# Where a division and an inverse root stand in a TensorE-bound transformer block

## The chip, the cores and the metric

The kernel runs on one core of one Trainium2 chip. The metric is the device time of one execution in microseconds, the median of several runs. A core has TensorE (PE, with its weight loads shown apart as PEld), VectorE (DVE), ScalarE (ACT) and GpSimd (POOL), each with an instruction queue that runs in order, and SyncE (SP), which here only issues transfers.

## The reference

A transformer block with conditioning, in fp32, on x of 4 sequences of 1024 tokens with 512 features; 16 heads of 32, a hidden width of 2048. `g` and `b` are linear in a conditioning vector of 128 per sequence.

```
norm(x) = g * x * rsqrt(mean(x*x) + 1e-6) + b
x1  = x + attention(norm1(x))          # softmax(q k^T / sqrt(32)) v, then Wo
ref = x1 + (silu(n @ gate^T) * (n @ hid^T)) @ out^T     with n = norm2(x1)
out = x + ref
```

What matters below: the softmax is divided by its row sums after the product with v, and norm2 needs the inverse root of one mean per token.

## The kernel before

Everything is held transposed: features on the 128 partitions, tokens along the rows. Tokens come in 8 blocks of 512 (two to a sequence). For each block there are 4 groups of 4 heads and 2 halves of 256 queries: 64 jobs `j`. A job takes 4 slots, each for 256 of the 1024 keys. So the main loop (L774) runs over 256 slots `g` plus 12 to drain, 32 slots to a block; `kind` is g mod 4, and in this text a slot's *place* is g mod 32.

The order of the work is written out by hand: inside the loop each engine's instructions stand in the order in which the calls are made, and the scheduler leaves the four compute engines alone. SyncE's transfers are placed by the framework. Three lists hang further work into slots: `pin` at a slot's start, `between` and `amid` in its middle, `after` at its end.

A job is a pipeline over several slots. `scores` (L316) puts a slot's scores into PSUM; `keep` (L323, ACT) copies them out; `running_max` (L328, L331, DVE) takes the maxima. At the next slot of kind 0, `max_T` (L337) transposes the maxima and `parts` (L343 to L348, DVE) reduces them to one per query. At the slot of kind 1 behind it, `parts_T` (L353, tile pt, then a copy L355) turns them, and `spread` (L363, tile sp, then copies L364 to `shift`) puts them on all partitions. `shifted` (L369, DVE) subtracts, `exponential` (L372, ACT) takes exp in place, one slot later `weighted` (L382, tile av) multiplies with v, and `accumulate` (L396) adds the slot's exponentials to the job's first by a transfer that GpSimd issues. When a job's four are summed, at the next slot of kind 0, `fold_sum` (L404) and `sums` (L414) give the row sums, `sums_out` (L419) copies them out as `total`, `inverse` (L422) takes their reciprocal on VectorE and `normalize` (L431) multiplies the job's output by it into oT.

From slot FS = 60 on, the feed-forward part (FFN) runs beside the attention of the next blocks, one hidden group `p` to two slots. Its products are pairs into two PSUM banks, a (tile pa) and b (tile pb): `pair_26`, `filler` (the output product pc of earlier groups, 4 x 512 columns), `pair_7` in even slots; `pair_3`, `pair_15` of the next group and `pair_4` in odd ones. On VectorE `take_contract` (L583) adds pc to the residual in `res`, which frees pc's bank; `sub_5` (L552) and `add_15` (L530) combine products; `gate` and `hidden` make h. Tiles pa, pc, sum, pt and sp all come from the pool `ps`, tag w, which has two banks.

The second norm of a block (tag f) takes squares (L138 to L144), a mean over features by TensorE (`norm_mean`, in the slot e + 17), and then an inverse root on few values: each of 512 tokens has one value on all 128 partitions, so `compact` writes one row to DRAM, `take` reads it back as 128 x 4 (tile few), `root` (L173, ACT, Sqrt) and `invert` (L177, DVE) work on that, and `put` and `norm_spread` bring it back to all partitions through DRAM. `norm_scale` (L199) and `norm_mod` (L202) then scale x. e is the block's first slot for block 0, and four slots before it for the others, so that e + 20 is place 20 there and place 16 here.

The diff touches the end of the loop's body, where a job is divided:

```
906            if n_on and j_n < direct and kind in (0, 2):
909                at = g - kind
910                in_first = j_n % GB == GB - 1 or (at >= FS and at % BS not in (12, 24, 28))
911                if in_first == (kind == 0):
912                    inverse(j_n)
914                    if j_n != GB:
915                        normalize(j_n)
```

j_n is the job whose sums are due, GB = 8 jobs and BS = 32 slots to a block. In the FFN's slots this puts the division into the slot of kind 0, but two slots later for the jobs due at places 12, 24 and 28 (so at places 14, 26 and 30). The last two jobs are divided in `take_sums`.

Of the kernel before, what the change touches and what calls it, by code (L numbers as in the profile page):

```python
# [9 lines left out]

F32 = mybir.dt.float32
BF16 = mybir.dt.bfloat16
AF = mybir.ActivationFunctionType
ALU = mybir.AluOpType
# [3 lines left out]
P = 128  # L18
# [6 lines left out]
def tile_cond_transformer_block(  # L25
# [13 lines left out]
    nc = tc.nc  # L39
    NBLK, _, C, _ = x.shape  # L40
# [17 lines left out]
    sb = ctx.enter_context(tc.tile_pool(name="sb", bufs=1))  # L58
# [14 lines left out]
    eps = const.tile([P, 1], F32, tag="eps", name="eps")  # L73
# [42 lines left out]
    y, wkq, wv, wo, kq, v = {}, {}, {}, {}, {}, {}  # L116
# [3 lines left out]
    state = {}  # L120
# [30 lines left out]
    def norm_mean(tag: str, inside: bool):  # L151
        if inside:
            pm = ps_av.tile([P, NB], F32, tag="av", name=f"pm{tag}")
        else:
            pm = ps.tile([P, NB], F32, tag="w", name=f"pm{tag}")
        mm(pm, ones_mean, state[tag], True, True)
        nc.scalar.copy(state[tag], pm)

    def compact(tag: str, t, rows: int, n: int):

# [3 lines left out]
    def take(tag: str):  # L164

        src = inv_s.pop(tag)
        few = sb.tile([P, src.shape[0] * src.shape[1] // P], F32, tag="few", name=f"few{tag}", bufs=2)
        nc.sync.dma_start(out=few, in_=src.rearrange("h (p c) -> (h p) c", c=few.shape[1]))
        state["few", tag] = few

    def root(tag: str):
        few = state["few", tag]
        nc.scalar.activation(few, few, AF.Sqrt, bias=eps)  # L173

    def invert(tag: str):
        few = state["few", tag]
        nc.vector.reciprocal(few, few)  # L177

    def put(tag: str):
        few = state.pop(("few", tag))  # L180
# [144 lines left out]
    def running_max(r: int, k: int):  # L325
        j, u = divmod(r, UN)
        if u:
            nc.vector.tensor_tensor(rmax[j], rmax[j], raw[r][:, k, :, :], ALU.max)  # L328
        elif k:
            rmax[j] = sb.tile([P, HG, HQ], F32, tag="rmax", name=f"rmax{j}")  # L330
            nc.vector.tensor_tensor(rmax[j], raw[r][:, 0, :, :], raw[r][:, 1, :, :], ALU.max)  # L331
# [74 lines left out]
    def take_av(j: int):  # L406
        avs[j] = sb.tile([P, HQ], F32, tag="avs", name=f"avs{j}", bufs=2)
        nc.scalar.copy(avs[j], av.pop(j))
# [12 lines left out]
    def inverse(j: int):  # L421
        nc.vector.reciprocal(state["total", j], state["total", j])  # L422

    def normalize(j: int):

        m, qh = divmod(j, NB // HQ)
        n, hg = divmod(m, C)
        total = state.pop(("total", j))
        if (n, hg) not in oT:
            oT[n, hg] = sb.tile([P, NB], F32, tag=f"oT{hg}", name=f"oT{m}")  # L430
        nc.vector.tensor_tensor(oT[n, hg][:, qh * HQ : (qh + 1) * HQ], avs.pop(j), total, ALU.mult)  # L431
# [157 lines left out]
    GB = C * (NB // HQ)  # L589
    BS = GB * UN  # L590
# [15 lines left out]
    def after(g, fn, *a):  # L606
        ended.setdefault(g, []).append((fn, a))
# [21 lines left out]
    for b in range(1, B):  # L629
        for half in range(QB):  # L630
            s = math.ceil((len(queue) + 1) / PACE)
            s4 = s - 4 - (s - 6) % UN
            tag = f"a{b}_{half}"
# [10 lines left out]
    FS = BS + 28  # L644
# [3 lines left out]
    for n in range(NBLK):  # L648
        g0 = (n + 1) * BS
        pin(g0 + 6, load_res, n)  # L650
        e = g0 if n == 0 else g0 - 4
        go = e + 13 if n < NBLK - 1 else g0 + 8
        for d in range(C):
            first.append((go, None, project_out, (n, d)))
            pin(go - 3 + (d // 2 * 4 if n else 0), load_wo, n, d)
        if n < NBLK - 1:
            tag = f"f{n}"
            after(e + 16, add_res, n)
            for k in range(2):
                after(e + 15 + k, lambda n=n, tag=tag, k=k: norm_squares(x2[n], tag, k))  # L660
            if n == 0:
                between(e + 17, norm_mean, tag, False)
            else:
                amid.setdefault(e + 17, []).append((norm_mean, (tag, True)))
            after(e + 17, norm_compact, tag)
            after(e + 19, take, tag)
            after(e + 20, root, tag)
            after(e + (20 if n == 0 else 21), invert, tag)
            after(e + (21 if n == 0 else 22), put, tag)
            after(e + (22 if n == 0 else 24), norm_spread, tag)  # L670
            scales, mods = ((24, 24, 25, 25), (25, 25, 26, 26)) if n == 0 else ((22, 22, 24, 24), (23, 23, 25, 25))
            for c in range(C):
                after(g0 + scales[c], lambda n=n, tag=tag, c=c: norm_scale(x2[n], tag, c))
                between(g0 + mods[c], lambda n=n, c=c: norm_mod(1, n // QB, x2[n], c))
            for i in range(4):
                after(g0 + (26, 26, 27, 28)[i] - (n > 0 and i == 0), token_sums, n, i)
# [27 lines left out]
    with tc.manual_schedule(  # L704
# [69 lines left out]
        while g < END:  # L774
# [40 lines left out]
                keep(g)  # L815
            if kind == 1 and s_on:
                take_av(j_s)
            due = bool(first) and first[0][0] <= g
            if not ffn:
                if x_on:  # L820
                    exponential(r_x)
                evict = chain(g, FG)
                if kind == 0:
                    take_sums(j_n)
                if g < NR:
                    running_max(g, 0)
                    running_max(g, 1)
                if kind == 0 and m_on:
                    columns[0] = P
                    max_T(j_m)  # L830
                    parts(j_m)
                if evict is not None:
                    evict()
                for fn, a in halfway.pop(g, []):
                    fn(*a)
                if g == FS - 1:
                    columns[0] = DH
                    pair_15(0)
                    take_5(0)
                    add_15(0)  # L840
                elif even:
                    late = chain(g, FG)
                if g in (FS - 4, FS - 2):
                    load_f((g - FS + 4) // 2)
            elif even:
                load_f(p + 2)
                pair_26(p)
                copy_156(p)
                if kind == 0:
                    take_sums(j_n)  # L850
                if x_on:
                    exponential(r_x)
                if kind == 0 and m_on:
                    max_T(j_m)
                    parts(j_m)
                one, two, evict = filler(p)
                one()
                two()
                if g < NR:
                    running_max(g, 0)  # L860
                    running_max(g, 1)
                if evict is not None:
                    evict()
                pair_7(p)
                sub_5(p)
                for fn, a in halfway.pop(g, []):
                    fn(*a)
            else:
                extra = due or len(queue) > FG
                evict = None  # L870
                if kind == 3 and extra:
                    evict = chain(g)
                pair_3(p)
                if kind == 3:
                    gate_tanh(p)
                if x_on:
                    exponential(r_x)
                pair_15(p + 1)
                take_5(p + 1)
                for fn, a in amid.pop(g, []):  # L880
                    fn(*a)
                if kind == 1:
                    gate_tanh(p)
                    if extra:
                        spare_bank[0] = True
                        evict = chain(g)
                if g < NR:
                    running_max(g, 0)
                if kind == 3 and evict is not None:
                    evict()  # L890
                if kind == 3:
                    gate(p)
                if g < NR:
                    running_max(g, 1)
                add_15(p + 1)
                if kind == 1:
                    gate(p)
                    if evict is not None:
                        evict()
                pair_4(p)  # L900
                hidden(p)
                if due:
                    chain(g)()
                for fn, a in halfway.pop(g, []):
                    fn(*a)
            if n_on and j_n < direct and kind in (0, 2):


                at = g - kind
                in_first = j_n % GB == GB - 1 or (at >= FS and at % BS not in (12, 24, 28))  # L910
                if in_first == (kind == 0):
                    inverse(j_n)

                    if j_n != GB:
                        normalize(j_n)
            columns[0] = DH
            for fn, a in ended.pop(g, []):
                fn(*a)
# [93 lines left out]
```

## Time and profile before

| | us |
|---|---|
| median of 3 runs (lowest, highest) | 2449.82 (2447.05, 2451.08) |
| the profiled execution | 2455.29 |
| its span in the trace | 2453.4 |
| four slots from place 4 on in the FFN (slots 100 to 103) | 29.6 |
| mean granted TensorE clock | 0.994 |

A slot's length is the distance of the first score matmul (L316) from the one of the slot before. In the profile, lines are those of the kernel before. A row of the timeline gives start and length in us, engine, line, operation, the tiles it writes and reads, and how many instructions are merged; brackets hold the idle time of that engine before it and what ended it. The start-up before the first slot takes 50.5 us; the FFN's tail without attention runs from about 2190 to the end.

### The profile page before, as it was taken

What the parts mean: (1) busy time and instruction counts of PE and PEld (TensorE: products, weight loads), DVE (VectorE), ACT (ScalarE), POOL (GpSimd) and SP (SyncE); (2) the same over time, 40 slices, a digit from 0 to 9 for tenths busy, and PEclk for the clock granted to TensorE, in tenths of its full rate; (3) what the DMA queues carried; (4) which work ended last, traced back from release to release, by engine and by line L of the source; (5) the groups of instructions that cost most, each with busy time, mean ns of one, the idle gap of its engine ahead of it and who ended that gap; (6) DMA issues with size and microseconds to landing.
All of it is one profiled execution on the core that took longest, in us unless ns stands there. A gap on an engine that the chain in (4) does not pass through costs nothing. (4 is left out here: it accounts for less than half of the span.)

```text
span 2453.4 us, 72677 instructions
## 1 busy us (share of the span) xinstructions
PE 2385.5 (97%) x32553; PEld 1135.9 (46%) x32553; DVE 1940.7 (79%) x2183; ACT 1413.2 (58%) x1495; POOL 172.4 (7%) x207
## 2 busy tenths in 40 slices
PE   8999999999999999999999999999999999999999
PEld 3333334344444544544454544454445445444444
DVE  2688888878799988998899979997999799843332
ACT  3677776765566656665566656665666566512110
POOL 0000000000000000000000000000000000000000
PEclk9999999999999999999999999999999999999999
DMA  6599999988788788889888888898788888853442
GB/s 216 166 304 259 256 258 240 231 202 219 198 205 210 188 226 209 208 207 229 204 200 213 225 197 209 204 230 207 198 207 203 224 200 204 198 165 117 140 131 70
DMA packets 185988, 501.79 MB, mean 205 GB/s; under 512 B 21319, under 2 KB 78663, under 8 KB 158286
## 3 DMA queue, kind: packets, MB, share of 16 engines
q0 software_dynamic: 28656, 208.68, 43.9%
q1 hardware_dynamic: 156734, 288.47, 35.4%
q8 instruction: 256, 4.19, 0.7%
q14 instruction: 54, 0.44, 0.1%
q10 hardware_dynamic: 288, 0.01, 0.0%
HBM read 246.44 MB, written 41.97 MB: 118 GB/s over the span
## 5 line engine op out<-in xcount | busy, mean ns | idle before, releaser
L369 DVE TENSOR_TENSOR raw<-raw,shift 128x2048 f32<-128x2048 f32 (+1 forms) x320 | 588.8, 1857 | 25.6 <-ACT shift L364 25.6
L323 ACT COPY raw<-sc 128x2048 f32<-128x2048 f32 x256 | 479.7, 1874 | 187.4 <-PE sc L316 130.8
L372 ACT ACTIVATE raw<-raw 128x2048 f32<-128x2048 f32 x256 | 490.8, 1917 | 157.1 <-DVE raw L369 154.8
L328 DVE TENSOR_TENSOR rmax<-rmax,raw 128x1024 f32<-128x1024 f32 x384 | 469.5, 1223 | 48.8 <-ACT raw L323 42.2
L112 PE MATMUL pc<-h,ow 128*32 128x512 f32 x4096 | 470.5, 596 | 5.2 <-DMA ow<-in_out_w 4.2
L382 PE MATMUL av<-raw,v 128*32 128x256 f32 x4096 | 271.9, 383 | 35.6 <-ACT raw L372 35.1
L396 POOL DMA_DIRECT2D raw<-raw x192 | 165.3, 861 | 1967.4 <-ACT raw L372 878.9
L316 PE MATMUL sc<-q,k 32*128 32x256 f32 x4096 | 293.3, 400 | 1.0 <-ACT raw L323 1.0
L112 PE MATMUL pa<-x,fa 128*32 128x256 f32 x4096 | 272.5, 384 | 4.1 <-DVE pa L530 4.1
L112 PE MATMUL pa<-sums,fw 128*32 128x256 f32 x4096 | 271.5, 383 | 0.0
L112 PEld LDWEIGHTS pc<-h,ow 128*32 128x32 f32 x4096 | 128.6, 110 | 250.7 <-issue 231.9
L316 PEld LDWEIGHTS sc<-q,k 32*128 32x128 f32 x4096 | 184.9, 184 | 117.4 <-issue 75.8
L112 PE MATMUL pkq<-y,wkq 128*32 128x512 f32 (+1 forms) x1664 | 232.5, 594 | 4.3 <-ACT y L202 4.1
L112 PEld LDWEIGHTS pa<-x,fa 128*32 128x32 f32 x4096 | 124.7, 110 | 119.7 <-DVE pa L530 21.4
L382 PEld LDWEIGHTS av<-raw,v 128*32 128x32 f32 x4096 | 110.4, 109 | 149.4 <-ACT raw L372 66.0
L112 PEld LDWEIGHTS pa<-sums,fw 128*32 128x32 f32 x4096 | 134.4, 111 | 90.0 <-issue 3.4
L583 DVE SCALAR_TENSOR_TENSOR res<-pc,res 128x512 f32<-128x512 f32 x128 | 88.2, 689 | 78.9 <-PE pc L112 76.2
L545 ACT COPY pb<-pa 128x256 f32<-128x256 f32 x128 | 46.1, 360 | 174.4 <-PE pa L112 173.3
L562 ACT ACTIVATE t<-pa 128x512 f32<-128x512 f32 x128 | 78.1, 610 | 109.9 <-PE pa L112 109.6
L112 PE MATMUL pb<-x,fw 128*32 128x256 f32 x2048 | 134.0, 379 | 1.2 <-ACT pb L545 1.2
L112 PE MATMUL pa<-x,fw 128*32 128x256 f32 x2048 | 134.0, 379 | 0.0
L552 DVE TENSOR_TENSOR pb<-pb,p 128x256 f32<-128x256 f32 x128 | 55.0, 430 | 99.8 <-PE pb L112 94.2
(108 smaller groups left out, 2243.7 us busy)
## 6 DMA issues: line engine op xcount, KB each, us to landing
raw<-raw POOLq DMA_DIRECT2D x192, 1024.0 KB, 9.3
fw<-sw SPq DMA_DIRECT2D x128, 512.0 KB, 7.8
fa<-in_gh_w SPq DMA_DIRECT2D x128, 384.0 KB, 6.8
ow<-in_out_w SPq DMA_DIRECT2D x128, 256.0 KB, 3.1
wkq<-in_kq_w SPq DMA_DIRECT2D x32, 512.0 KB, 6.2
v<-vs SPq DMA_DIRECT2D x128, 128.0 KB, 6.6
k<-kqs SPq DMA_DIRECT2D x124, 128.0 KB, 6.5
kqs<-st SPq DMA_DIRECT2D x61, 256.0 KB, 8.3
```

Source lines behind the costliest of these rows:

```text
L112: nc.tensor.matmul(dst[k : k + n, :], w[:, k : k + n], moving, start=start, stop=stop, skip_group_check=seeded)
L316: nc.tensor.matmul(sc[:, i, k, :], keys[rows, k * P : (k + 1) * P], queries[rows, :], start=True, stop=True)
L323: nc.scalar.copy(raw[r].rearrange("p k h q -> p h k q"), state.pop(("sc", r)))
L328: nc.vector.tensor_tensor(rmax[j], rmax[j], raw[r][:, k, :, :], ALU.max)
L369: nc.vector.tensor_tensor(t, t, s.unsqueeze(1).to_broadcast(list(t.shape)), ALU.add)
L372: nc.scalar.activation(raw[r], raw[r], AF.Exp)
L382: nc.tensor.matmul(av[j][i * DH : (i + 1) * DH, :], v[m, u][:, k, i * DH : (i + 1) * DH], raw[r][:, k, i, :], start=(kt == 0), stop=(kt == ...
L396: nc.gpsimd.dma_start(out=acc[j].rearrange("p k h q -> p (k h q)"), in_=raw[r].rearrange("p k h q -> p (k h q)"), accum_op=ALU.add,)
L545: nc.scalar.copy(bank_b[p][:, RIGHT], bank_a[p][:, RIGHT])
L552: nc.vector.tensor_tensor(b[:, LEFT], b[:, RIGHT], fifth.pop(p), ALU.subtract)
L562: nc.scalar.activation(state["t", p], bank_a[p], AF.Tanh, scale=0.5)
L583: nc.vector.scalar_tensor_tensor(r, pp, 0.5, r, ALU.mult, ALU.add)
```

## The change

First, `divide` is the block of lines 906 to 915 as a function. Slots without FFN call it where it stood. Even FFN slots call it behind the running maxima and ahead of the eviction of pc (the residual), so ahead of `pair_7`, `sub_5` and what `halfway` holds too. TensorE's own order is the same in both programs; VectorE's differs in this move and in the place of one small instruction.

Second, the root of the second norm leaves ScalarE. The copy of the mean adds eps. `inverse_root` starts from a guess by a shift and an exclusive or on the bits (one VectorE instruction), scales it, and takes four Newton steps of four GpSimd instructions each. In GpSimd's queue these 17 stand behind the transfer of slot e + 21; `take` is where it was. For the blocks from 1 on e + 21 is place 17, `put` and `norm_spread` stay in their slots; in block 0 both move one slot back, to 54 and 55.

```diff
@@ norm_mean
-        nc.scalar.copy(state[tag], pm)
+        nc.scalar.activation(state[tag], pm, AF.Identity, bias=eps)
@@ take
-        few = sb.tile([P, src.shape[0] * src.shape[1] // P], F32, tag="few", name=f"few{tag}", bufs=2)
+        few = sb.tile([P, src.shape[0] * src.shape[1] // P], F32, tag="few", name=f"few{tag}")
@@
-    def root(tag: str):
+    def inverse_root(tag: str):
+
         few = state["few", tag]
-        nc.scalar.activation(few, few, AF.Sqrt, bias=eps)
-
-    def invert(tag: str):
-        few = state["few", tag]
-        nc.vector.reciprocal(few, few)
+        y, t = (sb.tile(list(few.shape), F32, tag=f"few{i}", name=f"few{i}{tag}") for i in range(2))
+        nc.vector.tensor_scalar(
+            y.bitcast(I32), few.bitcast(I32), 1, 0x3FFFFFFF, ALU.logical_shift_right, ALU.bitwise_xor
+        )
+        nc.gpsimd.tensor_scalar_mul(y, y, 1.35 * 2.0**62)
+        for _ in range(4):
+            nc.gpsimd.tensor_tensor(t, y, y, ALU.mult)
+            nc.gpsimd.tensor_tensor(t, t, few, ALU.mult)
+            nc.gpsimd.tensor_scalar(t, t, -0.5, 1.5, ALU.mult, ALU.add)
+            nc.gpsimd.tensor_tensor(y, y, t, ALU.mult)
+        state["few", tag] = y
@@ second norm, due slots
             after(e + 19, take, tag)
-            after(e + 20, root, tag)
-            after(e + (20 if n == 0 else 21), invert, tag)
-            after(e + (21 if n == 0 else 22), put, tag)
-            after(e + (22 if n == 0 else 24), norm_spread, tag)
+            after(e + 21, inverse_root, tag)
+            after(e + 22, put, tag)
+            after(e + (23 if n == 0 else 24), norm_spread, tag)
@@ main loop
+            def divide():
+
+                if n_on and j_n < direct and kind in (0, 2):
+                    at = g - kind
+                    in_first = j_n % GB == GB - 1 or (at >= FS and at % BS not in (12, 24, 28))
+                    if in_first == (kind == 0):
+                        inverse(j_n)
+
+                        if j_n != GB:
+                            normalize(j_n)
+
...
                 if g < NR:
                     running_max(g, 0)
                     running_max(g, 1)
+                divide()
                 if evict is not None:
                     evict()
                 pair_7(p)
...
-            if n_on and j_n < direct and kind in (0, 2):
-
-
-                at = g - kind
-                in_first = j_n % GB == GB - 1 or (at >= FS and at % BS not in (12, 24, 28))
-                if in_first == (kind == 0):
-                    inverse(j_n)
-
-                    if j_n != GB:
-                        normalize(j_n)
+            if not ffn:
+                divide()
```

More of the change, by code (lines that the diff above doesn't have):

```diff
@@ L11 @@
 F32 = mybir.dt.float32
+I32 = mybir.dt.int32
 BF16 = mybir.dt.bfloat16
```

## The prediction

> **What bounds the kernel.** I read the page from the top: busy shares first, then the row of the granted clock, then the timeline of single slots.
>
> ```profile
> PE 2385.5 (97%) x32553; PEld 1135.9 (46%) x32553; DVE 1940.7 (79%) x2183; ACT 1413.2 (58%) x1495; POOL 172.4 (7%) x207
> ```
>
> TensorE (PE) is busy 97% of the span, so work taken from another engine is worth nothing by itself. Only a wait of PE that goes, or one that comes, moves the end. The groups by line say which of the touched work is large: 64 divisions (L422, 1744 ns each) and 64 multiplications by them (L431, 425 ns) on VectorE, 7 table loads (L173, 1283 ns) with 7 loads back on ScalarE. So I looked at the slots in which these stand. First, a slot of kind 0 with a division (slot 100) and the start of the slot behind it, in the timeline (start, length, engine, line, op, and in brackets the idle time before it with its releaser):
>
> ```profile
> 860.70 1.22 DVE L331 TENSOR_TENSOR rmax<-raw 128x1024 f32<-128x1024 f32 x1
> 862.08 1.05 PE L112 MATMUL pb<-x,fw 128*32 128x256 f32 x16
> 862.33 0.69 DVE L583 SCALAR_TENSOR_TENSOR res<-pc,res 128x512 f32<-128x512 f32 x1 [0.41 <-PE pc L112]
> 863.07 0.27 PE L353 MATMUL pt<-ident_bf,split 128*32 128x128 bf16 x2
> 863.26 0.43 DVE L552 TENSOR_TENSOR pb<-pb,p 128x256 f32<-128x256 f32 x1 [0.24 <-PE pb L112]
> 863.27 1.15 PE L316 MATMUL sc<-q,k 32*128 32x256 f32 x16
> 863.60 1.74 DVE L422 RECIPROCAL total<-total 128x256 f32<-128x256 f32 x1
> 864.86 0.58 ACT L364 COPY shift<-sp 128x512 f32<-128x512 f32 x1 [1.12 <-PE sp L112]
> 865.38 0.43 DVE L431 TENSOR_TENSOR oT<-avs,total 128x256 f32<-128x256 f32 x1
> 865.72 2.35 DVE L369 TENSOR_TENSOR raw<-raw,shift 128x1024 f32<-128x1024 f32 x2
> ```
>
> The residual (L583) empties the bank of pc at 863.02, and 0.05 us later PE starts pt, the first matmul of the next slot. Both use the pool with two banks (tag w), the other of which pa holds; in the order of the built program the matmul of pt waits for this very L583. The profile books no wait here, since the residual ends as PE comes free. PE is in order, so sc and everything behind it stand behind pt. The division (863.60) lies after that, beside sc, sp and av. VectorE has 0.41 us to spare ahead of the residual and 0.24 ahead of L552, no more.
>
> **The move of the division.** It goes ahead of the residual in all FFN slots that divide. The pair takes from 863.60 to 865.81, 2.21 us; an instruction that needs nothing of the one before starts 0.09 ahead of that one's end (865.72 against 865.81). So in slot 100 the maxima end at 861.92, the pair then at 861.92 - 0.09 + 2.21 = 864.04, and the residual at 864.04 - 0.09 + 0.69 = 864.64 instead of 863.02: pt starts **1.62 us later**. In slot 112 VectorE comes to the residual with only 0.10 us to spare (967.24 after maxima that end at 967.15), so 967.15 + 2.71 = 969.86 instead of 967.93, **1.93 us later**. Is it given back? The next slot's exp follows from pt through sp, the copies L364 and keep, and av of the slot after starts 0.05 us after that exp ends (870.39 to 870.44): the whole chain hangs on pt, PE has no slack to absorb it, and I count it in full.
>
> How often: kind-0 slots from 64 on divide unless their place in the block of 32 is 12, 24 or 28. Slots 64 and 68 have no cost (in 64 no pc stands, in 68 the residual waited 7.5 us for PE). Of the rest, 17 (places 4, 8, 20) look like slot 100 and 11 (places 0, 16) like slot 112; in slot 256 there are no maxima and 1.22 us to spare, so about 0.85. Sum: 17 x 1.62 + 11 x 1.93 + 0.85 = **+49.6 us**.
>
> The other 19 FFN divisions (places 14, 26, 30) have no pt behind them; there the bank is wanted by pair_15, about 2.4 us into the next slot. At place 14 the residual would end at 953.83 against 954.78: free, and VectorE fills its 0.36 us of waits, reaching L369 0.54 us sooner (954.08). At place 16 PE waits 0.28 us for exp and 0.20 for L530, both behind that L369; its slots take 10.71 against 9.91 elsewhere. Worth 0.54 x 6 = **-3.2**. At place 30 it fits (1076.19 + 2.71 = 1078.90 against pair_15 at 1079.23), and at 26 pair_15 is 0.3 late, which the longer wait of place 28 swallows: 0. If that cover went, 6 x 0.3.
>
> **The root.** The load for Sqrt falls in a gap of ScalarE; the load back does not:
>
> ```profile
> 966.00 1.28 ACT L173 ACT_TABLE_LOAD   x1
> ...
> 973.51 1.28 ACT L372 ACT_TABLE_LOAD   x1
> 974.80 1.91 ACT L372 ACTIVATE raw<-raw 128x2048 f32<-128x2048 f32 x1
> ...
> 976.76 1.07 PE L382 MATMUL av<-raw,v 128*32 128x256 f32 x16 [1.39 <-ACT raw L372]
> ```
>
> av waits 1.39 us for an exp that starts 1.28 us late; slot 100's av waited for nothing. The same stands in six blocks (places 18), and with 1.45 us in slot 54. All 14 loads are gone in the changed order: 6 x 1.39 + 1.45 = **-9.8**. What is late next there is the exp itself, by 0.05.
>
> **The new chain.** Seventeen small GpSimd instructions, each waiting for the last, behind one VectorE instruction in the place of a 0.17 us reciprocal. No 128x4 arithmetic of GpSimd is in the trace. Bounds: 17 x 0.10 (its 128x1 memsets) = 1.7, and 17 x 0.86 (its transfer issues) = 14.6; nearest are the 0.20 and 0.28 of its 128x128 set-up, so 4.3 us. It starts about 979.1. Queued behind it on GpSimd are slot 18's transfer (983.50) and two that follow, and on SyncE the put, with a v load, the spread, ow, q and fw behind it. At 4.3 us it ends at 983.4: no cost. At 14.6 the transfers start 10 us late and the last lands about 1.2 us past the fold that needs it (1021.26): 7 x 1.2 = +8. The spread has from 981.75 to the scaling at 1014.05, the loads behind it serve slots of the next block and later; free in both cases. In block 0 put and spread move one slot, some 10 of 27 us spare. Identity with bias for the copy: 687 ns (L149) against 615 at most, 7 x 0.07 on ScalarE, hidden by its 58%.
>
> The Trainium skill, GPSIMD Engine Reference, section 8, speaks against the chain: GpSimd shares its SBUF interfaces with VectorE, and contends with instructions of two SBUF inputs, as L369 is. By it L369 of slot 18 could run longer; no row here shows it.
>
> **The clock.** A wait of this size can also cost clock. Windows over place 28, where PE waits 1.57 us for exp and then 0.2 more (length, busy times, PEclk, DMA share, GB/s):
>
> ```profile
> 1048.00:1057.00 9.00, 7.23 (x88) 3.51 (x81) 9.00 (x9) 4.62 (x5) 0.86 (x1) 0.81 1.03 265
> 1307.00:1316.00 9.00, 6.79 (x100) 3.44 (x96) 9.00 (x9) 4.67 (x5) 0.86 (x1) 1.00 1.04 267
> ```
>
> Granted clock 0.81 over 9 us is 3.4 us at half clock. Four of six such places have it, and these slots take 13.65 us instead of 12.60: 1.05 each. Waits up to 1.45 us never do (11 of them), nor do three single ones of 1.57 to 1.64. Bounds: none of the 28 new waits, 0; all, each 3.4 us at half, 28 x 1.7 = 48. I take two in five of the eleven longer and one in six of the shorter, 7 x 1.05 = **+7.4**. The Trainium skill, TensorE: Matmul & The Clock Gate, Why this matters for your kernels, asks for no idle gaps over about 3 us; by it this term would be 0 and the forecast 2486. The four rows above 1.5 us decide against it.
>
> **Sum.** 49.6 - 3.2 - 9.8 + 7.4 = +44. The profiled execution took 2455.29 (span 2453.4), 5.5 above the median 2449.82; such an execution would show 2499, and the median of runs goes to **2494 us**.
>
> **Rivals.**
> Faster: pt does not wait for the residual, because the bank or the order of VectorE leaves it free, and only the gains stay: 2450 - 13 = 2437. It decides if VectorE had 2.2 us to spare ahead of the residual; the rows show 0.41 and 0.10. For it: VectorE idles 76 us in all ahead of L583, but most of that in the tail. 0.04.
> Half absorbed: waits further on (place 28, place 0) take half of the 49.6, since VectorE or ScalarE catch up in PE's new waits: 2450 + 25 - 13 = 2462. Against: rmax of the slots between waits for keep, so VectorE starts each slot from PE anyway. 0.06, a third of it near no change.
> Clock everywhere: 2450 + 36.6 + 48 = 2534. For it: the new waits recur every 30 us; against: the single 1.57s. 0.07.
> The change falls short in its own part: GpSimd takes the upper bound, or the Identity brings loads of its own (the same function stands in L202 without one): 2494 + 8 to 10 = 2503. 0.05.
> The forecast itself: 0.78, from 2478 (no clock term, 8 less stall) to 2518 (half of the waits at half clock).
>
> The range 2474 to 2522 leaves out the faster case, most of the half-absorbed one and the clock everywhere. Bound of what a measurement can tell: 0.2%, 5 us. Faster 0.04, same 0.03, slower 0.93.
>
> **What would show it.** pt starts 0.05 us after L583 in the new order, 1.6 to 1.9 us after the last pair_7, 28 times, with PE idle put down to VectorE's residual; L422 directly behind L331. No loads at the root, no wait of av at place 18. Half-clock stretches of 3.4 us behind some pt. GpSimd's chain ends ahead of its next transfer. I am wrong if pt comes on time, if the time lost at pt is missing later as shorter waits, or if the spread lands after the scaling wants it.

## The result, and the profile after

Four runs of the changed kernel have a median of 2528.19 us (2524.85 to 2531.21), against 2449.82 for the kernel before on the same chip: a ratio of 1.0322, with a 95% interval of 1.0301 to 1.0342. It is slower by 78.4 us, and 34 us over the forecast, outside its range. (A fourth, disturbed run of the kernel before, of 3478 us, is left out of its median.) The profiled execution took 2527.23 with a span of 2525.4, 72.0 more than the span before; the rest of the 78.4 is the 5.5 by which the profile of before lay above its median, and the 1.0 by which the profile of after lay below its own. Lines are those of the changed kernel in this part (L591 was L583, L404 was L396, and so on).

First the busy times. TensorE has 18 us more, at the same number of instructions: it ran part of the time at a lower clock (granted on average 0.988, against 0.994 before). GpSimd has 93 us more for 119 more instructions, 0.78 each.

```profile
PE 2403.3 (95%) x32553; PEld 1139.3 (45%) x32553; DVE 1938.0 (77%) x2183; ACT 1392.8 (55%) x1474; POOL 265.8 (11%) x326
```

Then the waits: who waited for whom, us in total, times, and the longest.

```profile
PE pt L361 <- DVE res L591: 48.1, 29, 1.9
ACT raw L331 <- DMA raw<-raw: 41.4, 9, 7.4
...
PEld pb L113 <- ACT pb L553: 28.1, 7, 5.0
...
PE pb L113 <- ACT pb L553: 21.8, 7, 4.1
```

The first row is new, and it is the one that the prediction worked out: 29 times, 48.1 us. The second is new too (0.2 us once, before), and the prediction has nothing of it: ScalarE's `keep`, the copy of the scores, waits for a transfer. The last two rows say what hangs on it: the copy L553 is late, and with it PE's `pair_7`. Before, each of them had one wait, of 2.1 and 1.2.

The distance of the slots' first score matmuls, after less before, puts the whole time in place. (A place stands here for the stretch from its slot's first score matmul to that of the next slot.) The slots from 64 on (six blocks) sum to +74.2; the slots ahead of them have -1.4, what follows -0.1, the start-up -0.6.

| place | each, us | sum | what it is |
|---|---|---|---|
| 4, 8, 20 | +1.62 x 17 (at 68: -2.80) | +24.7 | pt behind the residual |
| 0 | +1.93 x 5 (at 64: -0.5) | +9.2 | the same, longer |
| 1 | +1.59 x 4 of 6 | +6.4 | half clock behind that longer wait |
| 16 | +1.48 x 6 | +8.9 | 1.93, less 0.45 that VectorE gives back |
| 18 | -1.41 x 6 | -8.5 | the table load that is gone |
| 22, 23 | +4.1 to 5.2, +0.5 to 2.1, x 6 | **+37.7** | not predicted |
| 27, 28 | +0.37; -0.37 or -1.41 | -4.2 | 0.37 moved on; less half clock in 4 of 6 |

Two of these rows differ as much between two executions of the same program. The profile of the chain in the tail (one of the experiments), whose program is the kernel before up to there, has -2.70 at slot 68 and -1.05 at four of the six places 28 against the profile of before. So -2.80 and the -1.04 in the four of place 28 are not shown to come from the change.

Slot 116 (place 20) in the timeline, the answer to slot 100 of before:

```profile
1007.27 1.22 DVE L339 TENSOR_TENSOR rmax<-raw 128x1024 f32<-128x1024 f32 x1
1008.41 1.74 DVE L430 RECIPROCAL total<-total 128x256 f32<-128x256 f32 x1
1008.65 1.05 PE L113 MATMUL pb<-x,fw 128*32 128x256 f32 x16
1010.19 0.42 DVE L439 TENSOR_TENSOR oT<-avs,total 128x256 f32<-128x256 f32 x1
1010.53 0.68 DVE L591 SCALAR_TENSOR_TENSOR res<-pc,res 128x512 f32<-128x512 f32 x1
1011.27 0.27 PE L361 MATMUL pt<-ident_bf,split 128*32 128x128 bf16 x2 [1.57 <-DVE res L591]
```

The pair stands between maxima and residual, the residual ends at 1011.21, and PE starts pt 0.06 later after 1.57 idle. At place 18 (slot 114), PE's av no longer waits; PE goes through without a gap:

```profile
985.39 1.93 ACT L380 ACTIVATE raw<-raw 128x2048 f32<-128x2048 f32 x1
986.25 1.15 PE L324 MATMUL sc<-q,k 32*128 32x256 f32 x16
987.38 1.07 PE L390 MATMUL av<-raw,v 128*32 128x256 f32 x16
```

So places 22 and 23 are the question. The chain of Newton steps runs in slots 114 to 116. A part of it beside VectorE, with the transfer that is queued behind it:

```profile
994.97 0.20 POOL L181 TENSOR_TENSOR few1f<-few0f 128x4 f32<-128x4 f32 x1
995.12 2.28 DVE L377 TENSOR_TENSOR raw<-raw,shift 128x2048 f32<-128x2048 f32 x1
995.24 2.21 POOL L182 TENSOR_TENSOR few1f<-few1f,fewf 128x4 f32<-128x4 f32 x1
...
997.51 1.23 DVE L336 TENSOR_TENSOR rmax<-rmax,raw 128x1024 f32<-128x1024 f32 x1
997.54 1.25 POOL L183 TENSOR_SCALAR few1f<-few1f 128x4 f32<-128x4 f32 x1
...
998.87 0.20 POOL L184 TENSOR_TENSOR few0f<-few0f,few1f 128x4 f32<-128x4 f32 x1
...
1005.38 0.91 POOL L404 DMA_DIRECT2D raw<-raw  x1 [0.31 <-issue]
```

L181 and L182 are the same operation on 128 x 4 values, and one takes 0.20 us, the other 2.21: it ends at 997.45, 0.05 behind VectorE's L377 (997.40). L183 ends 0.05 behind the maxima. The chain goes from 989.77 to 1005.07, 15.3 us, and the transfer starts 19.1 us after slot 114's first score matmul, where before it was 9.3. That is 9.85 us late. GpSimd issues the next transfers as the one before lands, 0.53 us later, so they are late as well. In the profile of before, the first score matmuls of slots 114 and 118, the three transfers, and `keep` of slot 118 stand so:

```profile
974.22 1.15 PE L316 MATMUL sc<-q,k 32*128 32x256 f32 x16
...
983.50 0.86 POOL L396 DMA_DIRECT2D raw<-raw  x1 [13.54 <-ACT raw L372]
...
993.59 0.86 POOL L396 DMA_DIRECT2D raw<-raw  x1 [9.24 <-DMA raw<-raw]
...
1002.22 0.86 POOL L396 DMA_DIRECT2D raw<-raw  x1 [7.77 <-DMA raw<-raw]
...
1005.27 1.15 PE L316 MATMUL sc<-q,k 32*128 32x256 f32 x16
...
1006.95 1.90 ACT L323 COPY raw<-sc 128x2048 f32<-128x2048 f32 x1
```

What the lateness does in slot 118 (place 22) of the changed kernel:

```profile
1017.51 1.15 PE L324 MATMUL sc<-q,k 32*128 32x256 f32 x16
...
1022.53 2.33 PE L113 MATMUL pc<-h,ow 128*32 128x512 f32 x20
...
1025.70 1.87 ACT L331 COPY raw<-sc 128x2048 f32<-128x2048 f32 x1 [6.36 <-DMA raw<-raw]
1026.13 0.85 POOL L404 DMA_DIRECT2D raw<-raw  x1 [10.50 <-DMA raw<-raw]
...
1027.46 0.38 ACT L553 COPY pb<-pa 128x256 f32<-128x256 f32 x1
...
1027.89 1.93 PE L113 MATMUL pb<-x,fw 128*32 128x256 f32 x16 [3.03 <-ACT pb L553]
```

`keep` wants to write the scores of slot 118 into the buffer of `raw` that the second of these transfers still reads: there are 10 such buffers, and in the built program slot 118 has the one of slot 110, whose exponentials that transfer adds up. Measured from slot 118's first score matmul, that transfer landed at -3.6 before, 5.3 ahead of `keep`; now it lands at 8.1, 11.7 later. 11.7 less 5.3 is 6.4, and 6.36 is ScalarE's wait. L553 stands behind `keep` on ScalarE and writes bank b, on which `pair_7` accumulates: 3.03 us idle on PE here, 3.0 to 4.1 in the six blocks. And then the clock falls. The window of 6.83 us from 1027.27 on (length, busy times of PE, PEld, DVE, ACT and POOL, granted clock, DMA share, GB/s):

```profile
1027.27:1034.10 6.83, 6.21 (x56) 2.99 (x60) 6.47 (x7) 4.27 (x4) 0.85 (x1) 0.50 1.06 246
```

`pair_7` takes 1.93 us for 16 matmuls instead of 1.05. Such a stretch stands in all six blocks (five of 6.83, one of 3.41), 37.6 us at half clock and so 18.8 lost; six waits make 20.6. Together 39, and places 22 and 23 have 37.7.

### The profile page after: what moved, and what is told of

It reads as the page before. It is cut to its first block, busy times and chain, and to the rows that moved or that the text cites. A ratio compares the mean times of both kernels' runs of the same rounds, so it can differ in the third digit from the quotient of the medians.

```text
span 2525.4 us, 72756 instructions
## 1 busy us (share of the span) xinstructions
PE 2403.3 (95%) x32553; PEld 1139.3 (45%) x32553; DVE 1938.0 (77%) x2183; ACT 1392.8 (55%) x1474; POOL 265.8 (11%) x326
## 5 line engine op out<-in xcount | busy, mean ns | idle before, releaser
L377 DVE TENSOR_TENSOR raw<-raw,shift 128x2048 f32<-128x2048 f32 (+1 forms) x320 | 589.6, 1858 | 95.3 <-ACT shift L372 95.3
L336 DVE TENSOR_TENSOR rmax<-rmax,raw 128x1024 f32<-128x1024 f32 x384 | 469.6, 1223 | 85.2 <-ACT raw L331 78.8
L404 POOL DMA_DIRECT2D raw<-raw x192 | 165.5, 862 | 1879.2 <-ACT raw L380 758.3
L324 PE MATMUL sc<-q,k 32*128 32x256 f32 x4096 | 301.0, 409 | 0.7 <-ACT raw L331 0.7
L390 PE MATMUL av<-raw,v 128*32 128x256 f32 x4096 | 279.4, 392 | 21.8 <-ACT raw L380 21.3
L113 PEld LDWEIGHTS pa<-x,fa 128*32 128x32 f32 x4096 | 123.4, 109 | 121.3 <-DVE pa L538 20.6
L113 PE MATMUL pb<-x,fw 128*32 128x256 f32 x2048 | 139.3, 391 | 21.8 <-ACT pb L553 21.8
L363 ACT COPY mT<-pt 12x256 bf16<-12x256 bf16 x64 | 23.2, 362 | 224.0 <-PE pt L361 224.0
L553 ACT COPY pb<-pa 128x256 f32<-128x256 f32 x128 | 46.2, 361 | 168.3 <-PE pa L113 167.2
L591 DVE SCALAR_TENSOR_TENSOR res<-pc,res 128x512 f32<-128x512 f32 x128 | 87.9, 687 | 64.2 <-PE pc L113 63.6
```

Of the source, the lines that this page charges most:

```text
L113: nc.tensor.matmul(dst[k : k + n, :], w[:, k : k + n], moving, start=start, stop=stop, skip_group_check=seeded)
L324: nc.tensor.matmul(sc[:, i, k, :], keys[rows, k * P : (k + 1) * P], queries[rows, :], start=True, stop=True)
L363: nc.scalar.copy(mT[j][:NP], pt[:NP, :, :].rearrange("p a b -> p (a b)"))
L377: nc.vector.tensor_tensor(t, t, s.unsqueeze(1).to_broadcast(list(t.shape)), ALU.add)
L390: nc.tensor.matmul(av[j][i * DH : (i + 1) * DH, :], v[m, u][:, k, i * DH : (i + 1) * DH], raw[r][:, k, i, :], start=(kt == 0), stop=(kt == ...
L404: nc.gpsimd.dma_start(out=acc[j].rearrange("p k h q -> p (k h q)"), in_=raw[r].rearrange("p k h q -> p (k h q)"), accum_op=ALU.add,)
```

## The experiments

The theory: the loss has two parts that have nothing to do with each other. The division puts a wait ahead of pt, as predicted. The chain on GpSimd is held by VectorE, delays the transfers queued behind it, and through the buffers of `raw` stops ScalarE and PE. The rival: places 22 and 23 are late because of the division's waits (VectorE or ScalarE behind), or by something else of the root's change (the order of the slots, the put, the new copy). Each run's median stands against the kernel before on its own chip: 2449.30 for the division alone, the root alone, half the chain and the division behind the residual, 2450.16 for the others.

**The division alone.** The kernel before, with `divide()` as in the change and the root on ScalarE.

> The division moved ahead of the residual, the root as in the kernel before. Theory A (the lost 78 us have two separate sources: pt waits for the residual in 28 slots, and the chain on GpSimd holds up the transfers of place 19 to 21): this kernel has the first alone, 17 x 1.62 + 11 x 1.93 less about 3 us at place 16, plus 2 to 6 half-clock stretches of 1.6 us behind the longer waits: 2450 + 46 + 6 = 2502, and places 22 and 23 as in the kernel before (8.10 and 5.53 us). Theory B (all of the loss follows from the division: its waits put VectorE, ScalarE and the clock out of step, which shows at place 22): about 2528 + 10 = 2538, with place 22 as long as in the changed kernel (12 to 13 us).

Measured: 2498.36 us, ratio 1.0197 (1.0182 to 1.0213). The same wait in its own profile:

```profile
PE pt L353 <- DVE res L583: 48.2, 29, 1.9
```

Places 22 and 23 are as before, and no row has `keep` waiting for a transfer. So the division accounts for the waits at pt and for nothing at places 22 and 23. None of its waits of 1.57 or 1.9 us brought half clock in this profile.

**The root alone.** The changed kernel with the division back at the end of the loop.

```diff
-                divide()
                 if evict is not None:
...
-            if not ffn:
-                divide()
+            divide()
```

> The inverse root by Newton's steps on GpSimd, the division where it stood. Theory A: the table loads go (-10), place 22 and 23 lose what they lose in the changed kernel (6.3 us in each of six blocks, 38 in all), with keep at place 22 waiting for the transfer that place 20 issued: 2450 - 10 + 38 = 2478. Theory B: only the gain, 2440.

Measured: 2486.05 us, ratio 1.0146 (1.0129 to 1.0163). The gain is there (-1.41 at place 18, six times), and so is the loss, +45.3 us at places 21 to 24:

```profile
ACT raw L331 <- DMA raw<-raw: 54.2, 15, 7.1
...
PEld pb L113 <- ACT pb L553: 25.8, 7, 4.7
...
PE pb L113 <- ACT pb L553: 19.5, 7, 3.8
```

The rival with the division is out. The two parts sum to 49.1 + 36.8 = 85.9 and together cost 78.4: with the division's waits in it, the loss at these places is 37.7 instead of 45.3, which is the difference, so the two parts are not wholly independent. `keep` shows where it is smaller: in this run it waits for a transfer at place 21 too (1.4 to 3.6 us in the six blocks), in the changed kernel 0.25 at most. That fits the 1.62 us by which the pt wait at place 20 moves the slots behind it back and the transfers not; no run tries it by itself.

One row of this profile bears on the clock. In slot 86, PE waits as long for L553 as in the changed kernel, and `pair_7` still runs at full speed:

```profile
751.61 1.07 PE L113 MATMUL pb<-x,fw 128*32 128x256 f32 x16 [3.13 <-ACT pb L553]
```

**Half the chain.** The changed kernel with two Newton steps instead of four, so nine GpSimd instructions; it leaves the two last steps of the iteration out. Everything else of the change stays.

```diff
-        for _ in range(4):
+        for _ in range(2):
```

> The changed kernel with two Newton steps in place of four: 9 GpSimd instructions for 17, so a coarser inverse root. Theory A: the chain ends about 7 us sooner, its three transfers start 7 us sooner, the second lands before keep of place 22 wants its buffer, and the 38 us at places 22 and 23 go: 2528 - 38 = 2490, with the waits of pt as they are. If the loss at place 22 came from the division, or from the late put and spread alone growing shorter by half: 2510 to 2528.

Measured: 2490.55 us, ratio 1.0167 (1.0152 to 1.0182). Places 22 and 23 are as before; the waits at pt stay. The last of the chain and the transfer behind it:

```profile
993.17 1.25 POOL L183 TENSOR_SCALAR few1f<-few1f 128x4 f32<-128x4 f32 x1
994.51 0.20 POOL L184 TENSOR_TENSOR few0f<-few0f,few1f 128x4 f32<-128x4 f32 x1
995.01 0.91 POOL L404 DMA_DIRECT2D raw<-raw  x1 [0.31 <-issue]
```

Nine instructions take 9.3 us, and the transfer starts 13.1 us after slot 114's first score matmul, 3.85 later than before; `keep` of place 22 then waits 0.9 to 1.7 us, which PE does not see. The length of the chain decides, not the order of the slots or the new copy. In this profile three of the pt waits at place 16 and one at place 0 brought half clock (+1.58 each, at places 17 and 1); in the changed kernel it was four at place 0.

**The chain without VectorE's long instructions.** What do 17 such instructions cost by themselves? The kernel before, with the same 17 on a constant tile in the FFN's tail, where VectorE runs no maxima and no subtraction of the shift; the result is not used.

```diff
+            if p == p0 + 6:
+                few = ones_mean[:, :4]
+                z, t = (sb.tile([P, 4], F32, tag="few", name=f"few{i}free", bufs=2) for i in range(2))
+                nc.gpsimd.tensor_scalar_mul(z, few, 1.35)
+                for _ in range(4):
+                    nc.gpsimd.tensor_tensor(t, z, z, ALU.mult)
...
```

> The kernel before, with 17 such GpSimd instructions on constant numbers in the FFN's tail, where nothing waits for them and VectorE's long instructions read one operand from PSUM. The hold by VectorE (theory A): each takes 0.20, with 0.08 between them, 17 x 0.28 = 4.7 us in all, none held. If the chain is slow by itself (its own dispatch, first use of the code, the semaphores between its parts): 10 to 15 us here too. Time of the kernel the same.

Measured: 4.7 us from 2158.74 to 2163.45 (the one run took 2454.11). Its instructions beside VectorE:

```profile
2159.33 0.20 POOL L970 TENSOR_TENSOR few1free<-few1free,ones_mean 128x4 f32<-128x4 f32 x1
2159.36 0.69 DVE L567 SCALAR_TENSOR_TENSOR h<-t,pa 128x512 f32<-128x512 f32 x1 [1.05 <-ACT t L562]
2159.62 0.20 POOL L971 TENSOR_SCALAR few1free<-few1free 128x4 f32<-128x4 f32 x1
2159.90 0.20 POOL L972 TENSOR_TENSOR few0free<-few0free,few1free 128x4 f32<-128x4 f32 x1
```

The starts lie 0.28 us apart, and a VectorE instruction that reads PSUM (pa) beside SBUF holds none of them. (VectorE is idle for 11 of the 17.) In the changed kernel 53 of 119 were held, all by VectorE instructions that read two inputs from SBUF: 26 by the maxima (L336), 20 by the subtraction L377, 6 by the fold (L412), 1 by L439. The 52 behind the first three end 0.05 to 0.09 us behind theirs. Of the 66 free ones 12 started with VectorE idle, 48 beside an instruction with an operand in PSUM (L591, L575, L578, L560, L538) and 6 beside the reciprocal L430, which takes 1.74 us but has one input. So it is the kind of VectorE instruction, not its length.

**The chain behind the transfers.** The root's change alone, all 17 instructions kept, in two halves: each is issued behind a transfer and in front of a gap in GpSimd's queue, and put and spread follow.

```diff
-            after(e + 21, inverse_root, tag)
-            after(e + 22, put, tag)
-            after(e + (23 if n == 0 else 24), norm_spread, tag)
+            for part in range(2):
+                after(e + (21 if n == 0 else 23 + part), inverse_root, tag, part, 2)
+            after(e + (22 if n == 0 else 24), rooted, tag)
+            after(e + (22 if n == 0 else 24), put, tag)
+            after(e + (23 if n == 0 else 25), norm_spread, tag)
```

> All 17 on GpSimd as in the changed kernel, but in two halves behind the transfers of place 19 and place 20, put behind the second and the spread a slot later; the division where it stood. In block 0 as in the changed kernel. Theory A: each half runs while a transfer is in flight (about 10 us), the transfers start at most 3 us late, keep of place 22 doesn't wait: 2440, with a chain as long as before in busy time and a put as late as in the changed kernel. If the late put and spread or the loads queued behind them on SyncE were the cause: 2478 or more.

Measured: 2443.67 us, ratio 0.9965 (0.9952 to 0.9979). Parts of GpSimd's row:

```profile
983.47 1.12 POOL L181 TENSOR_SCALAR few0f<-few0f 128x4 f32<-128x4 f32 x1 [6.68 <-DVE few0f L178]
984.67 2.09 POOL L184 TENSOR_TENSOR few1f<-few0f 128x4 f32<-128x4 f32 x1
...
988.52 0.20 POOL L187 TENSOR_TENSOR few0f<-few0f,few1f 128x4 f32<-128x4 f32 x1
989.00 0.90 POOL L409 DMA_DIRECT2D raw<-raw  x1 [0.28 <-issue]
...
992.19 0.20 POOL L187 TENSOR_TENSOR few0f<-few0f,few1f 128x4 f32<-128x4 f32 x1
996.55 0.89 POOL L409 DMA_DIRECT2D raw<-raw  x1 [4.17 <-DMA raw<-raw]
```

The same instructions take 8.9 us between a first and a last now, places 22 and 23 are clean, and the -1.41 at place 18 stays. With the run of the root alone this shows the theory's second half: the same 17 instructions in the same queue cost 37 us or save 6, by where they stand in it. Two things changed with the place: a transfer goes out between the halves, and VectorE holds 23 of the 119 instructions instead of 53. Which of the two does more was not tried. The put and the spread are later here than in the changed kernel, so their lateness is not what cost the 37.7.

**The chain on VectorE.** Three instructions a step on VectorE, in parts of one, two and one steps, in the slots e + 21 to e + 23, with put in e + 23.

```diff
+            nc.vector.tensor_tensor(t, y, y, ALU.mult)
+            nc.vector.scalar_tensor_tensor(t, t, -0.5, few, ALU.mult, ALU.mult)
+            nc.vector.scalar_tensor_tensor(y, t, 1.5, y, ALU.add, ALU.mult)
```

> The four Newton steps on VectorE instead of GpSimd (14 instructions of about 0.2 us, 5, 6 and 3 of them at the ends of places 17, 18 and 19), put one slot later, the division where it stood. Theory A: GpSimd's transfers stay on time, the table loads are gone: 2450 - 10 = 2440, and up to 6 more if the 1.3 us at place 18 reach the exp of place 19. If what cost 38 us was the later put and spread rather than GpSimd's transfers, part of it stays: 2450 to 2470.

Measured: 2455.56 us, ratio 1.0018 (1.0009 to 1.0027): a miss, since 2440 was expected. The transfers are on time and place 18 has its -1.41, but place 20 takes +1.15 in six blocks, and slot 58 6.5 more. Slot 116 has the +1.15 ahead of pc, in three steps:

```profile
991.22 1.07 PE L394 MATMUL av<-raw,v 128*32 128x256 f32 x16 [0.17 <-ACT raw L384]
...
992.49 1.07 PE L113 MATMUL pa<-x,fa 128*32 128x256 f32 x16 [0.20 <-DVE pa L542]
...
993.40 1.22 DVE L416 TENSOR_TENSOR raw<-raw 128x1024 f32<-128x1024 f32 x1
...
994.72 0.64 PE L426 MATMUL sum<-raw,ones_sum 128*32 128x256 f32 x8 [0.30 <-PE pa L113]
```

Measured from the slot's first score matmul, and against before, av starts 0.24 us later (its exp follows a late subtraction of the shift), the pair on pa 0.39 more (behind `add_15`, L542), and sum another 0.50: the fold L416 ends at 994.62, and sum starts 0.10 behind it (the row books this wait to PE itself). From there to pt and the next slot the distances are as before. So VectorE is behind with the work that slot 116 needs early. Nine small instructions (0.15 to 0.16 each, 0.20 apart) take 1.8 us of it in slots 115 and 116, and the wait at place 18 in which it used to catch up (1.27 us before) is gone. In block 0 the spread, one slot later than in the changed kernel, is issued at 504.61; the scaling that waits for it (VectorE idle 5.83) holds up the shift's subtraction, and av waits 4.05 for its exp.

**The division behind the residual.** The division alone, one call further down.

```diff
                 if evict is not None:
                     evict()
+                divide()
                 pair_7(p)
```

> The division between the residual and the product of pair_7 (VectorE: maxima, residual, reciprocal, multiplication, L552), the root as in the kernel before. If the bank of pc is what makes pt wait, pt starts 0.05 us after the residual as in the kernel before, nothing is lost, and at place 14 VectorE fills 0.24 us of waiting: 2450 - 1 = 2449, the same within 0.2%. If instead any division ahead of the end of the slot costs (because L552 or the division's own place is what pt or the next slot hangs on), most of the 49 us stay: 2490 or more.

Measured: 2446.16 us, ratio 0.9987 (0.9978 to 0.9996). The waits at pt are gone; place 16 has -0.34 six times. In the timeline the reciprocal follows the residual and the residual has its old 0.41 us of spare again:

```profile
994.55 0.69 DVE L583 SCALAR_TENSOR_TENSOR res<-pc,res 128x512 f32<-128x512 f32 x1 [0.41 <-PE pc L112]
995.16 1.74 DVE L422 RECIPROCAL total<-total 128x256 f32<-128x256 f32 x1
```

This is the first part's rule in one line of code: the same move, one instruction lower, costs nothing.

**Both, placed by these readings.** The chain behind the transfers, the division ahead of the residual in slots of kind 2 (where no pt follows) and behind it in those of kind 0.

```diff
+                if kind == 2:
+                    divide()
                 if evict is not None:
                     evict()
+                if kind == 0:
+                    divide()
```

> e8 with the division moved where it is free: ahead of the residual at places 14, 26 and 30, behind the residual (ahead of pair_7) in the slots of kind 0. Theory A: the gains alone, 2450 - 10 from the table loads - 3 from place 16 - 3 as in e3, 2434 to 2438. If placing both brings their waits back: above 2446.

Measured: 2438.26 us, ratio 0.9953 (0.9935 to 0.9971), 12 us under the kernel before. Place 16 has -0.47, place 18 -1.42, six times each, and no half clock is added. Its interval overlaps with that of the chain behind the transfers; that the second part helps is read from place 16, not from the medians. An eleventh buffer for `raw`, which would have tried the wait of `keep` directly, was not tried. What stands for it is that the wait goes with the landing: the second transfer landed 8.1, 2.6 and -1.8 us after slot 118's first score matmul in the changed kernel, with half the chain and with the chain behind the transfers, and `keep` there waited 6.36, 0.89 and not at all.

## Why the prediction was wrong

The sign held, and three of the five terms. The fourth, the clock, came out near its size by luck. The fifth, the chain, failed.

- **pt behind the residual, +49.6.** Right. 17 x 1.62 and 5 of the 11 x 1.93 show in the slots to the hundredth, the six at place 16 less what the next term gives back, and the waits view has 48.1 us in 29 waits, slot 256 among them. Nothing else of it was given back: the half-absorbed rival is out.
- **Place 16, -3.2.** Right: 6 x 0.45 = -2.7. At places 27 and 28 the 0.37 us of lateness came and was swallowed, as put.
- **The table loads, -9.8.** Right: 6 x 1.41 at place 18 and 1.41 in slot 54: -9.9.
- **The clock, +7.4.** Four stretches, 1.59 us each, +6.4; all behind the longer waits of place 0, none behind 17 waits of 1.57. Near in sum, but by luck: the same waits brought four stretches with half the chain, at other places, and none with the division alone. The split between longer and shorter waits was too even. The term rested on four of six waits at place 28 in one profile; in the profile of the chain in the tail, the same program up to there, none of these six brought half clock.
- **The chain, 0.** The profiled spans differ by 72 where 44 was forecast, and this term alone is off by 37.7. It is the step that failed: "At 4.3 us it ends at 983.4: no cost." It took 15.3, and cost 37.7. Two things were wrong in it. The duration came from GpSimd's set-up rows, in which VectorE does not run such instructions beside it; 4.7 us in the tail says that the value itself was right for a free GpSimd. And the upper bound, 14.6, was close to what happened, with the transfers 10 us late just as the text said, but it was priced by one reader only (the rival at 0.05 has that price, 2503): "the last lands about 1.2 us past the fold that needs it". The fold is the reader of the transfer's result. What was missed is the next writer of its source: `keep`, eight slots on, with 5.3 us to spare. With that one, 10 us late gives ScalarE a wait of 10 - 5.3 = 4.7 us in each of six blocks; passed on to PE in full that is 28 us, so 2522 before any half clock. Measured, PE waited 20.6 us for it and lost some 18.8 at half clock.

The rule of the Trainium skill on GpSimd that the prediction weighed was read the wrong way round: it let L369 run longer. L377, as it is now, takes 2.28 us, as before; GpSimd is the one that waits. The Trainium skill, SBUF — State Buffer, Who interferes with whom, says so: a VectorE instruction with two SBUF inputs and a GpSimd instruction that reads SBUF exclude each other for the whole instruction, and whichever comes second waits. The 52 ends at 0.05 to 0.09 us behind VectorE's agree with it, and so do the free ones beside one input or PSUM. The reverse, VectorE held by a 0.20 us instruction, cannot be told in these rows.

The other rule that it weighed (the Trainium skill, TensorE: Matmul & The Clock Gate, Why this matters for your kernels: no idle gaps over about 3 us) agrees with place 22, where all six waits of 3.0 to 4.1 us brought half clock. But four of the eleven waits of 1.9 us did so too, and in the run of the root alone one wait of 3.13 us did not; there the measurement decides.

## What to carry to other kernels

When work is put on a queue, price the lateness of what is queued behind it by all who wait for it: who needs the result, and who wants to write the buffer that it still reads. Take an operation's duration from rows in which its neighbours run too; a small GpSimd instruction lasted here until the VectorE instruction beside it ended, wherever that one read two inputs from SBUF. And before an instruction is put ahead of one that frees a PSUM bank, look who waits for that bank: one line lower it was free.

## What the runs showed of the hardware

- A GpSimd instruction on 128 x 4 fp32 values took 0.20 us, 0.28 from start to start in a chain; beside a VectorE TENSOR_TENSOR with both inputs in SBUF it lasted until 0.05 to 0.09 us behind its end, up to 2.21.
- VectorE's own 128 x 4 instructions took 0.15 to 0.16 us, 0.20 from start to start in a chain.
- In the changed kernel, PE waits of 3.0 to 4.1 us brought half clock each time (six of six, 3.41 or 6.83 us long), but one of 3.13 in the run of the root alone did not; waits of about 1.9 us in four, none and four of eleven in three profiles (the changed kernel, the division alone, half the chain); single waits of 1.57 us in none of 17 in each. The waits of 1.57 at place 28, followed by 0.2 more, brought it in four of six in the profile of before, and in none of six in that of the chain in the tail.
